# A two-layer gated transformer kernel on one core: a fold padded to full size, another order of memory pools, norms taken by four tiles, and another order of the last stores

## The chip, the cores and the metric

The kernel runs on one core of one Trainium2 chip. All data is fp32. The metric is the device time of one execution in microseconds (us), as the median over several runs. The profile is of one execution and gives the start, the length and the waits of each instruction on each engine: TensorE (PE, with its weight loads as PEld), VectorE (DVE), ScalarE (ACT), GpSimd (POOL) and SyncE (SP), which issues nearly all DMAs.

## The reference

The input x has 8 sequences of 256 rows and 1024 columns. Four sublayers follow one another, each with a layer norm before it and a gate `tanh(g)` behind it:

```python
x = x + tanh(g_xattn[0]) * autocorrelation(layernorm(x), ctx, ctx)     # 8 heads, FFT along the sequence
x = x + tanh(g_ffn[0])   * lora_ffn(layernorm(x), W, b, A, B, gate_w, gate_b)
x = x + tanh(g_xattn[1]) * attention(layernorm(x), ctx, ctx, mask, wq, wk, wv, wo)  # 32 query, 8 kv heads, rope
x = x + tanh(g_ffn[1])   * fourier_ffn(layernorm(x), W_base, b_base, enc0, enc1, coefs0, coefs1, mask0, mask1)
```

The last sublayer is linear in its input. It adds to `x @ W_base.T + b_base` a small-rank update: x goes through encoders of 32 and 8 rows, together 40, then through masked coefficients summed over three sets, and then through an inverse real Fourier transform along the 1024 output columns, all times 0.5. So its whole weight can be made once: `W_base.T + encr.T @ (0.5 * ws.T @ fourier)`, where `encr` is 40 x 1024, `ws` (the masked coefficients, summed) is 1024 x 40, and `fourier` is a constant 1024 x 1024 matrix.

## The kernel before, in words

The work is done in two passes of four sequences each (`NPASS`, `BP`). In a pass, x is held as eight tiles `xt` of 128 rows and 1024 columns (`TT`). The sublayers of a pass follow one another:

- `autocorrelation` does the first sublayer as products with transform matrices (`mats`, `inv`, `inv2`), in turns over sequences and halves of the columns. Beside it, as a generator that is advanced by `fill`, the program makes the keys and values of the attention for the pass (`keys_values`, stored to `kT_d` and `v_d`), and in pass 0, at its end, the weight of the last sublayer (`fold_last_layer`).
- `lora_ffn` does the second sublayer. `prepare` norms a tile (`normed`, L356), transposes it on TensorE (L366), copies it with ScalarE (L367) and multiplies it with the gate and the low-rank factor `ag` (L625).
- `attention` does the third in steps of a block of four tiles and a kv head. Block 0 is tiles 0 to 3, block 1 tiles 4 to 7; the outputs of block 1 (`outputs`, L954) are added to x until the very end of the sublayer.
- `fourier_ffn` does the last with the folded weight, two tiles at a time: `prepare` norms and transposes, `left` makes sums of operands, `project` makes the product of pair m (L1127) while pair m+1 is already prepared, and stores the two tiles. The second tile of a pair holds its rows in reversed order, so it is stored by an indirect DMA of GpSimd with row numbers (L1137); the first goes with a plain DMA of SP (L1136).

The large products use a seven-product scheme for blocks of two by two (`SEVEN`, `left_operands`, `right_operands`, `add_product`). `residual` (L371) adds a scaled product to x on VectorE.

`fold_last_layer` has two products. The first (L302) takes `ws` as its weight, 128 rows by 40 columns, with chunks `ft` of the Fourier matrix, into an accumulator of which 40 rows are used; ScalarE copies these to `dec` (L307). The second (L320) takes `encr` and `dec`, both with 40 rows, and VectorE adds the result to `W_base` (L327), makes the operands of the seven products (L333 to L336), and SP stores them to `w1_d`.

Memory is given out by pools. `big` holds buffers of 4 KB per partition in groups a, b and xn, seven of each, which all sublayers share in turn. Other tiles come from pools that a sublayer opens and closes like a stack: what a later sublayer opens lies at the addresses of what an earlier one closed, and a tile waits for the last reader or writer of the tile that was there. In the first stage of a pass the pools are opened in the order kv1, kv2 (keys and values), ac1, acw, ac2 (autocorrelation), so kv1 lies lowest; the low-rank sublayer's tiles then lie over kv1, kv2, ac1, acw and the start of ac2.

`norm_stats` takes mean and variance of a list of tiles (L349, L350), a root on ScalarE (L351) and a reciprocal (L352). In `fourier_ffn` it is called for tiles 0 to 3 and for tiles 4 to 7 before the first `prepare`.

The order of the instructions on an engine is not the program's. A scheduler decides it when the program is built: it takes what it reckons to be ready, earlier program text first. Each engine then executes its own list in that order, and waits for semaphores.

Of the kernel before, what the change touches and what calls it, by code (L numbers as in the profile page):

```python
# [11 lines left out]
F32 = mybir.dt.float32  # L12
U8 = mybir.dt.uint8
I32 = mybir.dt.int32
AF = mybir.ActivationFunctionType
# [4 lines left out]
P = 128  # L20
B, S, D = 8, 256, 1024
KC = D // P
NPASS = 2
BP = B // NPASS
TT = BP * S // P
HALF = 512
# [5 lines left out]
R1 = 40  # L32
NB = 512
NBT = NB // P
# [12 lines left out]
def flamingo_kernel(ctx: ExitStack, tc: tile.TileContext, a: dict, out: bass.AP):  # L47
    nc = tc.nc
# [4 lines left out]
    big = ctx.enter_context(tc.tile_pool(name="big", bufs=7))  # L53
# [54 lines left out]
    def big_tile(group, shape, name):  # L108
        return big.tile([P, *shape], F32, tag=group, name=name)
# [166 lines left out]
    def fold_last_layer(groups, pools):  # L276


        fp, ps_kv = pools
        group, wt_group = groups  # L280
        co = big_tile(group, [3, KC, R1], "co")
        mk = fp.tile([P, 3, KC, R1], U8, name="mk")
        for e in range(3):
            nc.sync.dma_start(co[:, e], a["coefs"][e].rearrange("(c p) r -> p c r", p=P))
            nc.sync.dma_start(mk[:, e], a["cmask"][e].rearrange("(c p) r -> p c r", p=P))
        encr = big.tile([R1, D], F32, tag=group, name="encr")
        nc.sync.dma_start(encr, a["encr"])
        both = big_tile(group, [2, KC, R1], "both")
        ws, mf = both[:, 0], both[:, 1]
        for e in range(3):  # L290
            nc.vector.tensor_copy(mf, mk[:, e])
            nc.gpsimd.tensor_mul(co[:, e], co[:, e], mf)
        nc.gpsimd.tensor_add(ws, co[:, 0], co[:, 1])
        nc.gpsimd.tensor_add(ws, ws, co[:, 2])
        yield
        dec = big.tile([R1, D], F32, tag=group, name="dec")
        accs = [ps_kv.tile([P, HALF], F32, tag="kv", name="acc") for _ in range(2)]
        for c in range(KC):
            ft = big_tile(group, [2, HALF], "ft")
            nc.sync.dma_start(ft, a["fourier"][c * P : (c + 1) * P, :])  # L300
            for h in range(2):
                nc.tensor.matmul(  # L302
                    accs[h][0:R1, :], ws[:, c, :], ft[:, h, :], start=(c == 0), stop=(c == KC - 1)
                )
            yield
        for h in range(2):
            nc.scalar.activation(  # L307
                dec[:, h * HALF : (h + 1) * HALF], accs[h][0:R1, :], AF.Copy, scale=0.5
            )
        for c in range(KH):  # L310
            wt = []
            for k in range(2):
                rows = slice((k * KH + c) * P, (k * KH + c + 1) * P)
                wt.append(big_tile(wt_group, [2, HALF], "w1in"))
                nc.sync.dma_start(wt[k], a["w1"][rows, :])
            for k in range(2):
                rows = slice((k * KH + c) * P, (k * KH + c + 1) * P)
                for h in range(2):
                    acc = ps_kv.tile([P, HALF], F32, tag="kv", name="acc")
                    nc.tensor.matmul(  # L320
                        acc,
                        encr[:, rows],
                        dec[:, h * HALF : (h + 1) * HALF],
                        start=True,
                        stop=True,
                    )
                    nc.vector.tensor_add(wt[k][:, h, :], wt[k][:, h, :], acc)  # L327
                if k == 0:
                    yield
            q = [[wt[k][:, j, :] for j in range(2)] for k in range(2)]  # L330
            t12, t47 = big_tile(group, [2, HALF], "w_t12"), big_tile(group, [2, HALF], "w_t47")
            nc.sync.dma_start(w1_d[0, :, c, :], q[0][0])
            nc.vector.tensor_sub(t12[:, 0, :], q[0][1], q[0][0])  # L333
            nc.vector.tensor_sub(t47[:, 1, :], q[1][1], q[0][1])
            nc.vector.tensor_sub(t12[:, 1, :], q[1][1], t12[:, 0, :])
            nc.vector.tensor_sub(t47[:, 0, :], t12[:, 1, :], q[1][0])  # L336
            for i, t in ((1, wt[1]), (3, t12), (5, t47)):
                nc.sync.dma_start(w1_d[i : i + 2, :, c, :].rearrange("r p d -> p r d"), t)
            yield
# [15 lines left out]
    def normed(dst, xt, mv, rstd, i):  # L355
        nc.vector.tensor_scalar(  # L356
            dst, xt, mv[:, i, 0:1], rstd[:, i : i + 1], ALU.subtract, ALU.mult
        )
# [731 lines left out]
    def fourier_ffn(p, xt, groups):  # L1090
        with (
            tc.tile_pool(name="f1c", bufs=1, reuse_waits="tile") as w1,
            tc.tile_pool(name="f1", bufs=2, reuse_waits="tile") as w2,
            tc.tile_pool(name="f1_t", bufs=4, space=PSUM) as ps_t,
            tc.tile_pool(name="f1_o", bufs=4, space=PSUM) as ps_o,
        ):
            w = stored_weight(groups, lambda r: w1_d[WEIGHTS.index(r)])

            bias1 = w1.tile([P, D], F32, name="bias1")
            nc.sync.dma_start(bias1, a["b1"].partition_broadcast(P))  # L1100
            nc.vector.tensor_scalar(bias1, bias1, tg_f[1], None, ALU.mult)
            norms = [norm_stats(xt[i * NBT : (i + 1) * NBT]) for i in range(TT // NBT)]

            def prepare(t):
                xn = w2.tile([P, D], F32, tag="xn", name="xn")
                normed(xn, xt[t], *norms[t // NBT], t % NBT)
                xnT = w2.tile([P, KC, P], F32, tag="xnT", name="xnT")
                transposed(xnT, xn, ps_t, "t")
                return xnT

            def left(first, second):
                q = [[s[:, k * KH : (k + 1) * KH, :] for k in range(2)] for s in (first, second)]
                s = [w2.tile([P, KH, P], F32, tag=f"s{i}", name=f"s{i}") for i in (1, 2, 4)]
                return left_operands(nc.vector, q, *s)

            def project(m, ops):
                x = [
                    [xt[m * 2 + i][:, j * HALF : (j + 1) * HALF] for j in range(2)] for i in range(2)
                ]
                part = [w2.tile([P, HALF], F32, tag=f"part{i}", name=f"part{i}") for i in range(2)]  # L1120

                for i in range(2):
                    nc.vector.tensor_add(xt[m * 2 + i], xt[m * 2 + i], bias1)
                for r in SEVEN:
                    po = ps_o.tile([P, HALF], F32, tag="o", name="po")
                    for c in range(KH):
                        nc.tensor.matmul(  # L1127
                            po,
                            ops[r][:, c, :],
                            w[r].chunk(c),  # L1130
                            start=(c == 0),
                            stop=(c == KH - 1),
                        )
                    add_product(r, po, x, tg_f[1], ntg_f[1], part)
                b = p * BP + m
                nc.sync.dma_start(out[b * S : b * S + P, :], xt[m * 2])  # L1136
                nc.gpsimd.indirect_dma_start(  # L1137
                    out,
                    bass.IndirectOffsetOnAxis(ap=rows[:, b : b + 1], axis=0),
                    xt[m * 2 + 1],  # L1140
                    None,
                )

            pending = None
            for m in range(TT // 2):
                got = left(prepare(m * 2), prepare(m * 2 + 1))
                if pending is not None:
                    project(*pending)
                pending = (m, got)
            project(*pending)  # L1150

    for p in range(NPASS):
        ga, gb = ("a", "b") if p % 2 == 0 else ("b", "a")
        xt = [xpool.tile([P, D], F32, tag="x", name="x") for t in range(TT)]
        with (
            tc.tile_pool(name="kv1", bufs=1, reuse_waits="tile") as kw1,
            tc.tile_pool(name="kv2", bufs=2, reuse_waits="tile") as kw2,
            tc.tile_pool(name="ac1", bufs=1, reuse_waits="tile") as c1,
            tc.tile_pool(name="acw", bufs=1, reuse_waits="tile") as aw1,
            tc.tile_pool(name="ac2", bufs=2, reuse_waits="tile") as aw2,  # L1160
            tc.tile_pool(name="ac_dft", bufs=4, space=PSUM) as ps_dft,
            tc.tile_pool(name="ac_cor", bufs=1, space=PSUM) as ps_cor,
            tc.tile_pool(name="ac_out", bufs=1, space=PSUM) as ps_out,
# [28 lines left out]
        with tc.tile_pool(name="at_keep", bufs=1, reuse_waits="tile") as kp:  # L1192
            keep, norms, xops = [], {}, {}
# [163 lines left out]
```

## Time and profile before

| | |
|---|---|
| time, median of 3 runs | 3406.85 us (3405.84 to 3409.39) |
| profiled execution | 3400.72 us, of it 3399.0 us span |
| busy: PE, DVE, ACT, POOL | 3319.6, 2245.2, 859.5, 1355.3 us |
| mean granted clock of PE | 0.989 |
| DMA traffic | 431.72 MB, mean 127 GB/s |
| L302, first product of the fold | 32 instructions, 592 ns each, from 365.1 to 383.2 us |
| L320, second product of the fold | 32 instructions, 890 ns median (589 to 1219), from 385.6 to 412.9 us |
| pass 1 begins its keys on PE | at 1726.4 us |
| last matmul of the attention, pass 0 and pass 1 | 1616.5 and 3280.2 us |

The time of one instruction is from its start to its end; matmuls that follow one another overlap, so 16 instructions of 592 ns take 7.03 us. In a line of the timeline the bracket at the end tells how long the engine stood before it, and what released it. In a table of windows the column behind the five engines is the clock that TensorE was granted, 1.00 being full.

### The profile page before, as it was taken

The page shows a single profiled execution, that of the slowest core. Times are in us where ns is not written, and L with a number is a line of the kernel's source. Part 1 is how long each engine was busy: PE and PEld are TensorE (multiplying, and loading weights), DVE is VectorE, ACT ScalarE, POOL GpSimd, SP SyncE. Part 2 cuts the span into 40 slices and gives each one's busy share as a digit, 9 for nine tenths or more (in the row PEclk, how much of TensorE's full clock was granted, in tenths as well). Part 3 has the DMA queues.
Part 4 walks back from the last instruction along what each step waited for, and adds up shares of the span by engine and source line. Part 5 has one row for each costly group of instructions (what it writes and reads, how often), then busy time and mean ns, then how long its engine had stood idle before and what let it go on. Part 6 is the DMA issues. An engine that isn't in the chain of part 4 may idle for free. (4 is left out here: it accounts for less than half of the span.)

```text
span 3399.0 us, 36938 instructions
## 1 busy us (share of the span) xinstructions
PE 3319.6 (98%) x12784; PEld 2281.0 (67%) x12784; DVE 2245.2 (66%) x4229; ACT 859.5 (25%) x2061; POOL 1355.3 (40%) x1211
## 2 busy tenths in 40 slices
PE   8999999999999999999999999999999999999998
PEld 6676456777667767775467766577767777776754
DVE  7787666877777766665657775566666666666662
ACT  1332111322232322222123321122222323222220
POOL 4655212434443443445345541123443443344432
PEclk9999899999999999999999999999999999999999
DMA  7533625333333333343164333143333333333411
GB/s 273 172 115 117 213 87 176 118 137 133 139 126 129 121 119 120 121 163 103 50 203 153 126 102 131 32 158 123 123 121 121 113 123 115 121 123 122 152 38 50
DMA packets 161864, 431.72 MB, mean 127 GB/s; under 512 B 21476, under 2 KB 56292, under 8 KB 161678
## 3 DMA queue, kind: packets, MB, share of 16 engines
q1 hardware_dynamic: 160526, 425.17, 37.1%
q0 software_dynamic: 1152, 4.19, 0.3%
q8 instruction: 102, 1.67, 0.2%
q14 instruction: 84, 0.69, 0.1%
HBM read 350.66 MB, written 78.64 MB: 126 GB/s over the span
## 5 line engine op out<-in xcount | busy, mean ns | idle before, releaser
L719 POOL TENSOR_TENSOR qT<-rope,rope 128x512 f32<-128x512 f32 x128 | 170.0, 1328 | 866.9 <-DVE rope L718 866.9
L954 PE MATMUL po<-wo,oT 128*128 128x512 f32 x960 | 432.1, 593 | 0.0
L925 PE MATMUL ps_q<-xn,wq 128*128 128x256 f32 x1920 | 428.9, 379 | 0.0
L371 DVE SCALAR_TENSOR_TENSOR x<-po,tg,x 128x512 f32<-128x512 f32 x376 | 269.0, 745 | 201.3 <-PE po L954 70.6
L925 PEld LDWEIGHTS ps_q<-xn,wq 128*128 128x128 f32 x1920 | 364.8, 190 | 50.4 <-PE po L678 0.5
L987 ACT ACTIVATE s<-s,nmx 128x256 f32<-128x256 f32 x512 | 255.9, 500 | 276.5 <-DVE nmx L984 276.0
L982 DVE COPY_PREDICATED s<-keep,ps_s 128x512 f32<-128x512 uint8 x256 | 186.2, 730 | 183.0 <-PE ps_s L973 179.6
L954 PEld LDWEIGHTS po<-wo,oT 128*128 128x128 f32 x960 | 177.4, 190 | 175.6 <-issue 170.5
L954 PE MATMUL po<-wo,oS 128*128 128x512 f32 x640 | 287.7, 592 | 0.3 <-DVE x L371 0.3
L925 PE MATMUL ps_q<-xn_t,wq 128*128 128x256 f32 x1280 | 285.6, 379 | 0.0
L1014 ACT COPY wT<-pt 128x512 f32<-128x512 f32 x256 | 138.2, 590 | 516.3 <-PE pt L1008 516.0
L925 PEld LDWEIGHTS ps_q<-xn_t,wq 128*128 128x128 f32 x1280 | 243.2, 190 | 33.0
L1019 PE MATMUL av<-wT,v 128*128 128x256 f32 x1024 | 247.7, 384 | 3.8 <-ACT wT L1014 3.6
L973 PE MATMUL ps_s<-kT,qT 128*128 128x256 f32 x1024 | 247.9, 379 | 0.0
L1019 PEld LDWEIGHTS av<-wT,v 128*128 128x128 f32 x1024 | 192.5, 191 | 79.2 <-issue 44.0
L996 DVE TENSOR_SCALAR s<-s,tot 128x256 f32<-128x256 f32 x512 | 219.6, 469 | 7.7
L981 POOL MEMSET s<- 128x512 f32 x256 | 129.9, 527 | 222.2 <-PE pt L1008 220.5
L954 PEld LDWEIGHTS po<-wo,oS 128*128 128x128 f32 x640 | 119.0, 190 | 136.6 <-issue 128.9
L973 PEld LDWEIGHTS ps_s<-kT,qT 128*128 128x128 f32 x1024 | 191.6, 190 | 25.3 <-DVE x L371 0.5
L258 POOL TENSOR_TENSOR x<-x,part 128x512 f32<-128x512 f32 x80 | 114.9, 1436 | 213.5 <-ACT part L257 193.6
L984 DVE TENSOR_REDUCE nmx<-s 128x2 f32<-128x512 f32 x256 | 175.0, 685 | 8.3
L716 DVE TENSOR_TENSOR rope<-c,tab_q 128x512 f32<-128x512 f32 x128 | 88.4, 691 | 125.8 <-POOL c L240 119.9
(255 smaller groups left out, 5599.4 us busy)
## 6 DMA issues: line engine op xcount, KB each, us to landing
wq<-in_wq_dram SPq DMA_DIRECT2D x104, 512.0 KB, 3.3
wo<-in_wo_dram SPq DMA_DIRECT2D x104, 512.0 KB, 3.5
wq<-wq_d SPq DMA_DIRECT2D x96, 512.0 KB, 3.2
wo<-wo_d SPq DMA_DIRECT2D x96, 512.0 KB, 3.2
w<-w_d SPq DMA_DIRECT2D x36, 512.0 KB, 4.7
wk<-in_wk_dram SPq DMA_DIRECT2D x26, 512.0 KB, 5.8
wv<-in_wv_dram SPq DMA_DIRECT2D x26, 512.0 KB, 4.4
wk<-wk_d SPq DMA_DIRECT2D x24, 512.0 KB, 4.4
```

What stands on the lines that cost most here:

```text
L371: nc.vector.scalar_tensor_tensor(xs, ps, g, xs, ALU.mult, ALU.add)
L719: nc.gpsimd.tensor_add(dst, t0, t1)
L925: nc.tensor.matmul(ps[:, l, :], wops[r][:, l, c, :], xo[r][:, c, :], start=(c == 0), stop=(c == KH - 1),)
L954: nc.tensor.matmul(po, ops[r][:, h, t * P : (t + 1) * P], wops[r][:, h, :], start=(h == 0), stop=(h == 1),)
L973: nc.tensor.matmul(ps[:, t, :], qT[i, n][:, l, t * P : (t + 1) * P], kT[:, n * S : (n + 1) * S], start=True, stop=True,)
L981: nc.gpsimd.memset(s, MASKED)
L982: nc.vector.copy_predicated(s, keep[b], ps)
L984: nc.vector.tensor_reduce(nmx, s, AX.X, ALU.max, negate=True)
L987: nc.scalar.activation(s[:, t, :], s[:, t, :], AF.Exp, bias=nmx[:, t : t + 1], accum_out=tot[:, t : t + 1],)
L996: nc.vector.tensor_scalar(s[:, t, :], s[:, t, :], tot[:, t : t + 1], None, ALU.mult)
L1014: nc.scalar.copy(wT[i], pt)
L1019: nc.tensor.matmul(av[:, i, :], kv[step][1][:, n * 2 + c, :], wT[i][:, c, :], start=(c == 0), stop=(c == 1),)
```

## The change

It has four parts. In `fold_last_layer` the coefficients go into a zeroed tile `wide` of 128 columns per chunk, `encr` into a zeroed tile of 128 rows, and `dec` has 128 rows, so that both products of the fold are of 128 rows and 128 columns; the mask factors get a buffer of their own. In `fourier_ffn` the statistics are taken in `prepare`, for four tiles when the first of them is due. In `project` the scattered store is issued before the plain one. And the pools of the first stage are opened in another order, the autocorrelation's first, those of keys and values behind them. What is computed is unchanged.

```diff
-        encr = big.tile([R1, D], F32, tag=group, name="encr")
-        nc.sync.dma_start(encr, a["encr"])
-        both = big_tile(group, [2, KC, R1], "both")
-        ws, mf = both[:, 0], both[:, 1]
+
+        encr = big_tile(group, [D], "encr")
+        nc.gpsimd.memset(encr, 0.0)
+        nc.sync.dma_start(encr[0:R1, :], a["encr"])
+        wide = big_tile(group, [KC, P], "wide")
+        nc.gpsimd.memset(wide, 0.0)
+        ws = wide[:, :, 0:R1]
+        mf = big_tile(group, [KC, R1], "mf")
...
-        dec = big.tile([R1, D], F32, tag=group, name="dec")
+        dec = big_tile(group, [D], "dec")
...
-                    accs[h][0:R1, :], ws[:, c, :], ft[:, h, :], start=(c == 0), stop=(c == KC - 1)
+                    accs[h], wide[:, c, :], ft[:, h, :], start=(c == 0), stop=(c == KC - 1)
...
-                dec[:, h * HALF : (h + 1) * HALF], accs[h][0:R1, :], AF.Copy, scale=0.5
+                dec[:, h * HALF : (h + 1) * HALF], accs[h], AF.Copy, scale=0.5
...
-            norms = [norm_stats(xt[i * NBT : (i + 1) * NBT]) for i in range(TT // NBT)]
+            norms = {}
 
             def prepare(t):
+                if t % NBT == 0:
+                    norms[t // NBT] = norm_stats(xt[t : t + NBT])
...
-                nc.sync.dma_start(out[b * S : b * S + P, :], xt[m * 2])
                 nc.gpsimd.indirect_dma_start(
                     out,
                     bass.IndirectOffsetOnAxis(ap=rows[:, b : b + 1], axis=0),
                     xt[m * 2 + 1],
                     None,
                 )
+                nc.sync.dma_start(out[b * S : b * S + P, :], xt[m * 2])
...
-            tc.tile_pool(name="kv1", bufs=1, reuse_waits="tile") as kw1,
-            tc.tile_pool(name="kv2", bufs=2, reuse_waits="tile") as kw2,
             tc.tile_pool(name="ac1", bufs=1, reuse_waits="tile") as c1,
             tc.tile_pool(name="acw", bufs=1, reuse_waits="tile") as aw1,
             tc.tile_pool(name="ac2", bufs=2, reuse_waits="tile") as aw2,
+            tc.tile_pool(name="kv1", bufs=1, reuse_waits="tile") as kw1,
+            tc.tile_pool(name="kv2", bufs=2, reuse_waits="tile") as kw2,
```

## The prediction

> **What bounds the kernel now.** I read the page first, then the windows of five microseconds around each place where the clock or TensorE's busy share dips, then the timelines of TensorE, VectorE and GpSimd there.
>
> ```profile
> PE 3319.6 (98%) x12784; PEld 2281.0 (67%) x12784; DVE 2245.2 (66%) x4229; ACT 859.5 (25%) x2061; POOL 1355.3 (40%) x1211
> PEclk9999899999999999999999999999999999999999
> ```
>
> TensorE is busy for 3319.6 of 3399.0 us. A change that takes no matmul away can win only two things: the 79 us in which TensorE stands, and the time in which it runs at a lowered clock. The chain of waits says the same, nearly all of it is TensorE. So I looked for dips. The fifth slice is the only one with a granted clock below nine tenths:
>
> ```profile
> 375.00:380.00 5.00, 5.00 (x12) 1.41 (x11) 2.30 (x4) 0.00 (x0) 2.02 (x3) 1.00 0.29 105
> ...
> 400.00:405.00 5.00, 5.00 (x9) 2.38 (x9) 3.18 (x5) 0.00 (x0) 0.00 (x0) 0.50 0.60 230
> ...
> 410.00:415.00 5.00, 3.96 (x5) 1.11 (x4) 3.62 (x8) 0.00 (x0) 0.00 (x0) 0.50 0.70 263
> ...
> 420.00:425.00 5.00, 5.00 (x25) 5.00 (x25) 2.98 (x9) 1.73 (x4) 0.00 (x0) 0.50 1.02 328
> ```
>
> Columns: window, length, busy time of PE, PEld, DVE, ACT and POOL, then granted clock, DMA share, GB/s. From 400 us TensorE is busy all the time and yet gets half its clock. TensorE's timeline names what runs there (an fp32 matmul shows as two instructions):
>
> ```profile
> 378.45 5.34 PE L302 MATMUL acc<-ft,both 128*40 128x512 f32 x12
> ...
> 401.51 12.45 PE L320 MATMUL acc<-dec,encr 40*128 40x512 f32 x14
> 417.69 1.94 PE L366 MATMUL pt<-ident,xn 128*128 128x128 f32 x8 [3.73 <-DVE sc L636]
> ```
>
> The fold's first product, 128 rows by 40 columns, holds the full clock (0.44 us each). Its second, 40 rows by 128 columns, is in train when the clock falls (by windows of one microsecond between 398 and 399) and runs at 0.89 us each. Every other dip that I looked into follows a stand of 2.5 us or more; this one alone falls with TensorE busy.
>
> Next, three places where TensorE stands. The change of stage in pass 1, from the key and value projection to the low-rank layer:
>
> ```profile
> 2080.22 1.09 PE L366 MATMUL pt<-ident,xn 128*128 128x128 f32 x8 [1.56 <-DVE xa L640]
> 2085.92 3.68 PE L625 MATMUL pa<-ag,xnT 128*128 128x68 f32 x16 [4.61 <-ACT xnT L367]
> ```
>
> ```profile
> 2083.94 0.81 DVE L356 TENSOR_SCALAR xn<-x,mv,rstd 128x1024 f32<-128x1024 f32 x1 [3.77 <-DMA v_d<-v]
> ```
>
> The norm of tile 1 writes where the last v tile lay, so VectorE waits for its store; ScalarE's root and copies stand behind that, and TensorE behind them. The last layer of both passes starts with a stand too (pass 1 shown):
>
> ```profile
> 3280.85 0.73 DVE L371 SCALAR_TENSOR_TENSOR x<-po,tg,x 128x512 f32<-128x512 f32 x1
> 3281.50 1.28 DVE L349 BATCH_NORM_STATS2 st<-x 128x6 f32<-128x512 f32 x2
> ...
> 3282.81 0.76 DVE L356 TENSOR_SCALAR xn<-x,mv,rstd 128x1024 f32<-128x1024 f32 x1
> ...
> 3386.59 1.41 DVE L371 SCALAR_TENSOR_TENSOR x<-po,tg,x 128x512 f32<-128x512 f32 x2 [2.62 <-PE po L1127]
> 3390.03 0.75 DVE L371 SCALAR_TENSOR_TENSOR x<-po,tg,x 128x512 f32<-128x512 f32 x1 [2.02 <-PE po L1127]
> ```
>
> ```profile
> 3283.71 1.94 PE L366 MATMUL pt<-ident,xn 128*128 128x128 f32 x8 [3.55 <-DVE xn L356]
> 3285.52 2.07 PE L1127 MATMUL po<-w,xnT 128*128 128x512 f32 x2
> ```
>
> The norm of tile 0, whose own statistics were taken long before, sits behind statistics of tiles 4 to 7. And the end: the last residual is done at 3390.8, the plain store goes then, and the scattered store starts only when that has landed, 4.8 us before the span ends.
>
> ```profile
> 3394.21 0.97 POOL L1137 DMA_INDIRECT out_dram<-x,rows  x1 [11.17 <-DMA out_dram<-x]
> ```
>
> **The change part by part.** The sum is made against the profiled execution, 3400.72 us (span 3399.0 and 1.7 around it), which lies 6.1 us below the median of the runs, 3406.85.
>
> *Padding of the fold.* Rows of the second product go from 40 to 128, the columns of the first likewise. No matmul is added; 128 or 40 columns cost the same 592 ns row (L302 and L954), and the longer weight load (117 to 190 ns) lies beside a matmul of 512 columns. Two memsets of 128x1024 come to GpSimd, about 1.05 us each by the 527 ns of a 128x512 one; GpSimd idles 5.99 us before its add at 340.27, after the buffer of encr came free at 335.3. If that cover is gone they cost 2.1 us of GpSimd. One more big buffer is held (mask factors apart), so a fourier chunk may load a step later; the factors were ready at 350 and are used at 365. I cost these at nothing.
>
> What it may win is the clock. Half clock lasts from 398.6 to 425.4, 26.8 us with a stand of 3.7, so 11.5 us of TensorE's time are lost: upper end 12. Lower end: nothing, if the array's monitor does not count rows of zeros. Here a rule speaks against the change. The Trainium skill ("TensorE: Matmul & The Clock Gate", the parts on the clock gate and on why it matters) says that the gate goes by how busy the PE has been, and that a matmul with K=32 takes the time of one with K=128. By it 40 rows at 100% busy would hold the clock and padding would win 0. The rows above say that 40 rows at 5.00 of 5.00 got 0.50 while 128 rows by 40 columns got 1.00; the measurement decides, so I expect the full clock. Then VectorE is next: from 396.85 it has 22 fold operations of about 0.61 us and 0.6 us of small ones left, 14 us, and ends at 410.9 in place of 416.75. That is 5.9 us. The transposes and gate matmuls behind it (417.7 to 425.4, at half clock) win another 3.9 by the clock alone, but the copies and table load of ScalarE between them (1.28 us) then show; I count 1.6. Gain 7.5, bounds 0 and 12.
>
> *Pool order.* The low-rank layer's tiles now lie over the autocorrelation's pools, not over those of keys and values. Pass 1: their last reader is the matmul of L532 that ends at 2076.9, not the v store at 2083.9. Norm 0 can follow the residual (2078.4), norm 1 at once, transposes of both by 2081, root and copies by about 2082.4. What is late next is the load of ag, issued at 2079.89 behind the v store; by its row (5.4 us to landing) it is there at 2085.3, or at about 2082.5 if it is issued at 2077. So the gate matmuls come 1 to 3.5 us earlier, tile 1's transposes (1 us) fall into the wait, and of the 2.7 us lost to half clock behind the stand about half goes. I take 4.5, bounds 0 and 8. Pass 0: ag and bl now lie over the transform matrices, so they can't load at 371.6 but at about 389.5, after the last L532. SP issues nothing between 372.4 and 387.8, so nothing is queued behind; ag lands at 395 and the first use was at 394.88, in a stretch with DMA at 0.78 to 0.95. Loss 1, bounds 0 and 5. The start of pass 1 and attention: the same bottom addresses are covered as before; nothing.
>
> *Norms by four.* The stand and half clock at the start of the last layer cost 3.94 + 0.98 + 0.97 = 5.9 in pass 0 and 3.55 + 0.98 + 1.19 + 1.04 = 6.8 in pass 1 (transposes 1.94 against 0.96 for eight, products 1.85 and 2.07 against 0.88, transposes 2.95 against 1.91). With no statistics ahead of it norm 0 runs at 3279.3 or, behind the last residual, at 3281.6: TensorE stands 0.1 to 2.2 us, and about 0.6 us for the first copies. (A stand of 2.47 us before 613.9 was followed by half clock, one of 2.19 before 2051.7 was not, so I count none.) I leave 1.75 per pass: gain 12.7 - 3.5 = 9.2, bounds 4 and 12. The statistics of tiles 4 to 7 (eight of 0.65, four of 0.2, 6 us, and a root with its 1.28 us table load) must now fit before the transposes of tile 4 at 3314.2; VectorE idles about 8 us between 3298 and 3314, which hides them.
>
> *Scattered store first.* Its tile is ready at 3388.0 (second residual of the pair at 3386.59), the plain one at 3390.8. Both write the same tensor, so the second still waits: scatter lands at 3388.1 + 3.9 = 3392.0, plain store 3.4 later, 0.9 to the end: 3396.3 against 3399.0. Gain 2.7, bounds 0 and 3.9. SP now stands at the plain store instead of GpSimd at the scatter, about 2 us longer; behind it are pass 1's x, wk and ctx loads, whose first uses are 15 us or more away.
>
> Sum: 7.5 + 4.5 - 1 + 9.2 + 2.7 = 22.9, so 3377.8 for a like execution, 3384 for the median.
>
> **The rivals.** (a) *The clock stays halved*: zeros are not counted. For it: no row here shows a matmul padded with zeros. Against it: the fall with 40 rows, none with 40 columns. Sum 15.4: 3391.5. (b) *The orders hardly move*: what each engine issues first is fixed by a scheduler, and norm 0 may stay where it is because its tile opens late; then 3 us of the tail and little else remain, 3402. For it: VectorE had idle time from 3253 on and norm 0 did not use it. (c) *Slower*: norm 0 stays and the statistics of tiles 4 to 7 land directly in front of norm 4. Place: VectorE before the transposes at 1649.8 and 3314.2. Price: 6 of statistics, 1.6 on ScalarE, 1.2 for reciprocal and norm, some 3 of half clock, 11.8 per pass and 23.6 in all, against 13.7 from the other parts: 3417. It decides once more than 7 us per pass are exposed. Against it: 8 us of idle VectorE there.
>
> **How the numbers follow.** Main forecast 0.62, (a) 0.2, (b) 0.12, (c) 0.06. About 0.2% (6.8 us) is what a measurement of this kernel can tell from no change. The main case and (a) are faster, and a third of (b): 0.86; the rest of (b) is the same, 0.08; (c) 0.06. The range: all upper ends together (12, 8, 12, 3.9) would give 3371, which is unlikely at once; 3373 to 3398 holds the main case, (a), and the better edge of (b).
>
> **What would show it.** Right: L320 at 592 ns with 128 rows and a clock of 1.00 from 395 to 425; the norm of tile 1 in pass 1 without the wait for the v store; the first transposes of the last layer less than 2.5 us behind the last L954; the scatter near 3388 before the plain store. Wrong: L320 at 890 ns; gate matmuls in pass 0 waiting for ag; a stand before the transposes of tile 4.

## The result, and the profile after

The changed kernel takes 3390.79 us (median of 6 runs, 3386.70 to 3399.65), the kernel before in the same session 3407.11 (3405.84 to 3409.39). The ratio is 0.9959, 95% interval 0.9948 to 0.9969: 14.0 us less (11 to 18), where the prediction had 23. (The two medians are 16.3 us apart; I go by the ratio.) The time lies in the predicted range, but the sum behind it does not hold in all its terms. The runs after spread over 13 us, those before over 3.6. The profiled execution after took 3396.83 us, its span is 3395.0, so it is one of the long ones, while the one before (3400.72) is shorter than any of the six runs before. The two profiles are therefore only 3.9 us apart: they show where time went, and not the 14 us.

The page of the changed kernel, first the busy times, then the granted clock in 40 slices:

```profile
PE 3314.1 (98%) x12784; PEld 2279.1 (67%) x12784; DVE 2252.4 (66%) x4229; ACT 859.7 (25%) x2061; POOL 1354.6 (40%) x1213
PEclk9999999999999999999999999999999999999999
```

The dip in the fifth slice is gone, but TensorE's busy time fell by only 5.5 us. To see where the rest is, I cut the TensorE timelines of all profiled executions at the same matmuls. Kernels e1 to e12 are those of the experiments; times in us.

| stretch | before | after | e1 padding | e2 pools | e6 pools pass 0 | e8 | e10 |
|---|---|---|---|---|---|---|---|
| first matmul to first fold matmul | 359.2 | 368.2 | 360.4 | 369.5 | 367.4 | 362.0 | 361.0 |
| fold to last attention matmul, pass 0 | 1251.5 | 1249.0 | 1244.4 | 1262.3 | 1262.5 | 1245.5 | 1244.9 |
| last layer, pass 0 | 109.0 | 108.2 | 109.0 | 110.1 | 110.0 | 111.3 | 105.8 |
| to the last L532 matmul, pass 1 | 351.4 | 351.6 | 358.7 | 354.3 | 358.5 | 356.6 | 351.1 |
| to the first gate matmul, pass 1 | 9.0 | 5.4 | 8.8 | 4.8 | 9.0 | 5.2 | 5.2 |
| to the last attention matmul, pass 1 | 1194.2 | 1194.3 | 1194.2 | 1194.5 | 1195.4 | 1193.0 | 1194.6 |
| last layer, pass 1 | 109.8 | 107.3 | 109.8 | 108.6 | 108.8 | 105.6 | 107.3 |
| from the last matmul to the end | 9.0 | 5.3 | 9.0 | 9.0 | 9.0 | 5.3 | 5.3 |

The columns before and after differ in both directions: 9 us are lost ahead of the fold, five stretches win 1 to 4, and two (up to the last L532 matmul of pass 1, and its attention) do not move. A stretch of one execution is not exact either. From the fold to the attention, e3, e4 and e7, whose edits do not touch that stretch, take 1254.9 to 1255.9 us where the profile of before has 1251.5: the clock of the fold's second product falls 27 to 32 us after the first fold matmul there, and 33.5 in before. Up to the last L532 matmul of pass 1 the kernels lie between 349.7 and 358.7. I go through the stretches in the order of the prediction. In kernels that have the change, lines are 4 to 6 higher than before (in e11 by 2): L302 and L320 (fold) are L306 and L324, L366 is L370, L356 is L360, L371 is L375, L669 is L673, L1127 is L1133, L584 is L588.

*Fold.* Windows (columns as in the prediction: length, busy time of the five engines, then clock, DMA share, GB/s), and TensorE's timeline behind them:

```profile
400.00:405.00 5.00, 4.38 (x20) 2.58 (x20) 5.00 (x9) 1.08 (x2) 0.00 (x0) 1.00 0.89 277
410.00:415.00 5.00, 3.38 (x8) 1.05 (x7) 4.98 (x9) 0.00 (x0) 0.00 (x0) 1.00 1.02 376
```

```profile
414.92 2.33 PE L324 MATMUL acc<-dec,encr 128*128 128x512 f32 x4 [1.12 <-DVE w1in L331]
...
424.21 4.50 PE L673 MATMUL po<-w,xnT 128*128 128x512 f32 x6 [2.00 <-DVE w1in L331]
...
432.84 6.70 PE L673 MATMUL po<-w,xnT 128*128 128x512 f32 x8 [3.13 <-DMA w<-in_w_dram]
```

The clock is 1.00 through the second product, and VectorE is busy for 4.98 to 5.00 of 5 us: it is the next limit, as predicted. The last fourteen instructions of this product take 1057 to 1058 ns (median, from start to end) in all six profiles with 40 rows and 592 to 593 in all eight with 128. But then TensorE waits 2.00 us for a fold operation of VectorE and 3.13 us for the load of the next weight. Neither wait was there before.

*Pool order in pass 1.* TensorE's timeline:

```profile
2085.01 1.09 PE L370 MATMUL pt<-ident,xn 128*128 128x128 f32 x8 [0.50 <-DVE xn L360]
2088.18 3.65 PE L629 MATMUL pa<-ag,xnT 128*128 128x68 f32 x16 [2.08 <-DMA ag<-in_ag_dram]
```

The wait for the v store is gone, and the load of ag is what comes last, as predicted.

*Last layer, pass 1.* VectorE, then TensorE:

```profile
3282.55 0.69 DVE L353 BATCH_NORM_STATS2 st<-x 128x6 f32<-128x512 f32 x1
3283.17 0.73 DVE L375 SCALAR_TENSOR_TENSOR x<-po,tg,x 128x512 f32<-128x512 f32 x1
3283.82 1.53 DVE L360 TENSOR_SCALAR xn<-x,mv,rstd 128x1024 f32<-128x1024 f32 x2
```

```profile
3284.77 2.85 PE L370 MATMUL pt<-ident,xn 128*128 128x128 f32 x16 [2.29 <-DVE xn L360]
```

The norm now follows the last residual, with no statistics between them. The stand is 2.29 us in place of 3.55, and half clock still follows it (16 transposes in 2.85 us; at full clock they take 1.91).

*The end.* GpSimd's scatter, then SP's plain store:

```profile
3388.06 0.98 POOL L1142 DMA_INDIRECT out_dram<-x,rows  x1 [5.23 <-DVE x L375]
```

```profile
3391.45 0.33 SPq L1148 DMA_DIRECT2D out_dram<-x  x1
```

*Ahead of the fold.* One VectorE instruction that takes 0.43 us in the median, the end of GpSimd's work beside it, and the matmul that waits for what is queued behind it:

```profile
121.64 11.23 DVE L588 SCALAR_TENSOR_TENSOR w<-took,ex 128x256 f32<-128x256 f32 x1
```

```profile
130.05 2.54 POOL L158 TENSOR_TENSOR wv_s<-wv,wv_s 128x512 f32<-128x512 f32 x2
```

```profile
134.71 2.07 PE L536 MATMUL po<-re,inv 128*128 128x512 f32 x2 [6.79 <-DVE x L375]
```

That is most of the 9 us. No step of the prediction has anything at this place.

### The profile page after: what moved, and what is told of

Its sections match the earlier page's. It is cut to its first block, busy times and chain, and to the rows that moved or that the text cites. A ratio compares the mean times of both kernels' runs of the same rounds, so it can differ in the third digit from the quotient of the medians.

```text
span 3395.0 us, 36926 instructions
## 1 busy us (share of the span) xinstructions
PE 3314.1 (98%) x12784; PEld 2279.1 (67%) x12784; DVE 2252.4 (66%) x4229; ACT 859.7 (25%) x2061; POOL 1354.6 (40%) x1213
## 5 line engine op out<-in xcount | busy, mean ns | idle before, releaser
L375 DVE SCALAR_TENSOR_TENSOR x<-po,tg,x 128x512 f32<-128x512 f32 x376 | 269.1, 745 | 196.0 <-PE po L958 70.5
L258 POOL TENSOR_TENSOR x<-x,part 128x512 f32<-128x512 f32 x80 | 109.1, 1364 | 229.5 <-ACT part L257 222.1
L263 POOL TENSOR_TENSOR x<-x,part 128x512 f32<-128x512 f32 x80 | 104.7, 1310 | 172.7 <-DVE part L375 157.0
```

Source lines behind the costliest of these rows:

```text
L375: nc.vector.scalar_tensor_tensor(xs, ps, g, xs, ALU.mult, ALU.add)
```

## The experiments

All ratios are to the kernel before, run on the same chip in turn; 0.001 is 3.4 us.

**Each part alone (e1 to e4), on the kernel before.**

```diff
# e1: the hunks of the fold
...
+        wide = big_tile(group, [KC, P], "wide")
...
+        dec = big_tile(group, [D], "dec")
...
# e2: the hunk of the pools
-            tc.tile_pool(name="kv1", bufs=1, reuse_waits="tile") as kw1,
-            tc.tile_pool(name="kv2", bufs=2, reuse_waits="tile") as kw2,
             tc.tile_pool(name="ac1", bufs=1, reuse_waits="tile") as c1,
...
+            tc.tile_pool(name="kv1", bufs=1, reuse_waits="tile") as kw1,
+            tc.tile_pool(name="kv2", bufs=2, reuse_waits="tile") as kw2,
# e3: the hunk of prepare()
+                if t % NBT == 0:
+                    norms[t // NBT] = norm_stats(xt[t : t + NBT])
# e4: the hunk of project()
-                nc.sync.dma_start(out[b * S : b * S + P, :], xt[m * 2])
                 nc.gpsimd.indirect_dma_start(
...
+                nc.sync.dma_start(out[b * S : b * S + P, :], xt[m * 2])
```

> Only the padding of the fold, on the kernel before. Theory (read from the two traces): the clock is 1.00 from 398 to 425 us and L324 runs at 592 ns, but the last load of w1in is issued some 20 us later because one big buffer more is held, so the last fold additions and the first load of the next weight come late: 2 to 4 us are left, about 3404. Rival 1 (the step of the prediction): 7.5 us are won, about 3399.5, with no wait for a load behind the fold. Rival 2: the 9 us that the changed kernel lost ahead of the fold (one VectorE instruction of 11.23 us) come with the padding; then the first fold matmul is some 9 us later than before and the kernel is 5 us slower, 3412.

> Only the pool order, on the kernel before. Theory: in pass 1 the gate matmuls of the low-rank layer come about 2.4 us earlier against the last L532 matmul (the wait for the v store is gone, the load of ag is late next), and in pass 0 they come up to 1 us later: 1.5 to 2.5 us faster, about 3405. Rival 1 (the prediction): 4.5 - 1 = 3.5 faster, 3403.5. Rival 2: the buffers of the first stage lie elsewhere and VectorE's long instruction under GpSimd's train of additions at 121 to 133 us comes with this part: then the first fold matmul is 9 us later and the kernel is 6 us slower, 3413.

> Only the norms of the last layer by four tiles, on the kernel before. Theory (from the two traces): some of the statistics of tiles 4 to 7 stay ahead of the last residual, TensorE stands 2.3 to 2.8 us before the first transposes of the last layer in place of 3.5 to 3.9, and about 1 us in pass 0 and 2.5 us in pass 1 are won: 3.3 faster, 3403.5. Rival 1 (the prediction): 9.2 us, 3397.6, with stands under 2.2 us and the full clock behind them. Rival 2: nothing, as the scheduler puts the statistics where they were; 3407.

> Only the scattered store ahead of the plain one, on the kernel before. Theory (from the two traces): the tail behind the last matmul goes from 9.0 to 5.2 us, 3.8 us faster, 3403. Rival 1 (the prediction): 2.7 us, 3404.2. Rival 2: nothing at all, if the two stores share the queue's completion; 3407.

| run | median, us | ratio | 95% interval | us against before |
|---|---|---|---|---|
| e1 padding | 3397.45 | 0.9975 | 0.9965 to 0.9985 | -8.5 |
| e2 pools | 3408.98 | 1.0007 | 0.9998 to 1.0016 | +2.4 |
| e3 norms | 3403.03 | 0.9991 | 0.9982 to 0.9999 | -3.1 |
| e4 store | 3405.18 | 0.9994 | 0.9986 to 1.0002 | -2.0 |

The four add up to -11.2, inside the interval of the whole. The padding is worth about what the prediction gave it, not the 2 to 4 us that I read from the trace of after: my theory for e1 was wrong. For e2 it was wrong as well: its second rival, the long instruction, came, though +2.4 us is not clear of zero. e3 came out as its theory had it; e4 cannot tell 3.8 from 2.7. The late load that I had put down to the padding's extra buffer does not come with it. SP's queue in e1, then in after:

```profile
372.45 0.42 SPq L1211 DMA_DIRECT2D ag<-in_ag_dram  x1
...
393.25 0.34 SPq L319 DMA_DIRECT2D w1in<-in_w_dram  x1
```

```profile
397.66 0.38 SPq L1213 DMA_DIRECT2D ag<-in_ag_dram  x1
...
415.91 0.50 SPq L319 DMA_DIRECT2D w1in<-in_w_dram  x1
...
427.20 3.91 SPq L119 DMA_DIRECT2D w<-in_w_dram  x6
```

In e1 the last w1in load goes 27 us after the first fold matmul, in after 42 us. e2 has it late too (50 us), with no padding in it. So it belongs to the pool order, and so does the instruction of 11 us in the profiles: e2 has one of 11.53 us at 123.67, while e1, e3 and e4 have none there.

What the padding leaves: the fold's last wait is for VectorE, and a stand of 3.7 us behind it still drops the clock. TensorE and windows of e1:

```profile
411.59 1.94 PE L370 MATMUL pt<-ident,xn 128*128 128x128 f32 x8 [3.74 <-DVE sc L640]
```

```profile
405.00:410.00 5.00, 2.25 (x4) 0.59 (x4) 4.98 (x12) 0.00 (x0) 0.00 (x0) 0.98 1.02 379
410.00:415.00 5.00, 3.41 (x16) 3.22 (x16) 4.70 (x18) 2.26 (x4) 0.00 (x0) 0.50 1.01 345
```

**The pool order by pass (e6, e7), and the change without it (e5) or with it in pass 1 alone (e8).**

```diff
+        sizes = {"kv1": 1, "kv2": 2, "ac1": 1, "acw": 1, "ac2": 2}
+        order = list(sizes) if p == 1 else ["ac1", "acw", "ac2", "kv1", "kv2"]   # e6
+        order = list(sizes) if p == 0 else ["ac1", "acw", "ac2", "kv1", "kv2"]   # e7, e8
...
+                n: st.enter_context(tc.tile_pool(name=n, bufs=sizes[n], reuse_waits="tile"))
+                for n in order
```

> The changed kernel without the pool order (padding, norms by four and scattered store only). Theory (from the single runs: padding -8.5 to -9, norms -3.3, store -3.2 to -3.8, pool order +2.4): the pool order costs and does not win, so this is faster than the changed kernel: 3407 - 15 = 3392 or less, with the last w1in load where it was, no late load of the next weight and no VectorE instruction of 11 us at 122 us. Rival (the step of the prediction): the pool order wins 3.5, so this is slower than the changed kernel, 3394.5 by its measured 3390.8.

> Only the pool order, in pass 0 alone, on the kernel before. Theory: all of its cost lies here. The tile of ag opens late, the last w1in load is queued behind stores and goes some 20 us later, and the first load of the next weight behind that: from the first gate matmuls to the attention 6 to 8 us are lost; an 11 us VectorE instruction at 122 us may add 9. 3413 without, 3422 with. Rival (the prediction): 1 us lost, 3408.

> Only the pool order, in pass 1 alone, on the kernel before. Theory: what it wins lies here, 3.6 to 4.2 us between the last L532 matmul of pass 1 and the first gate matmul, and nothing before that differs: 3403. Rival 1 (the prediction): 4.5, 3402.5. Rival 2: the gain is given back in pass 1 as the cost is in pass 0: 3407.

> The changed kernel with the pool order in pass 1 alone. Theory: all gains without the cost in pass 0: 9 for the padding, 3.3 norms, 3.5 store, 4 pool order = 19.8 less than 3407: 3387, 4 us ahead of the changed kernel. Rival: the parts share their stands, so no more than the changed kernel, 3391.

| run | median, us | ratio | 95% interval | us against before |
|---|---|---|---|---|
| e5 change without pool order | 3395.50 | 0.9956 | 0.9943 to 0.9970 | -15 |
| e6 pool order, pass 0 alone | 3422.02 | 1.0030 | 1.0020 to 1.0040 | +10.2 |
| e7 pool order, pass 1 alone | 3404.24 | 0.9977 | 0.9967 to 0.9988 | -7.8 |
| e8 change, pool order in pass 1 alone | 3391.91 | 0.9942 | 0.9928 to 0.9955 | -19.8 |

(On this chip the kernel before ran at 3411.56; only the ratios compare with the first table.) One edit, two passes, opposite signs. The theory held for e6 and e8. For e7 the stretch to the first gate matmul is 5.0 us in place of 9.0, as expected; its ratio says more than these 4 us, but 4 is at the edge of its interval. e5 tells nothing against after (0.9956 and 0.9959), since the two halves of the pool order nearly cancel. In e6 the fold to the end of the attention takes 1262.5 us, in e7 1254.9: the late loads cost 7.6 us without padding (11.0 against the 1251.5 of before). With it they cost 3.6 (1249.0 in after, 1245.5 in e8). TensorE's stands for them in e6, which e7 does not have:

```profile
442.96 3.70 PE L669 MATMUL po<-w,xnT 128*128 128x512 f32 x8 [2.47 <-DMA w<-in_w_dram]
...
453.88 6.50 PE L669 MATMUL po<-w_t,s 128*128 128x512 f32 x8 [3.61 <-DVE w_t L140]
```

**Rows alone (e11).** The first product stays at 40 columns, the second gets 128 rows.

```diff
...
+        nc.gpsimd.memset(encr, 0.0)
...
+        nc.gpsimd.memset(dec, 0.0)
...
+                dec[0:R1, h * HALF : (h + 1) * HALF], accs[h][0:R1, :], AF.Copy, scale=0.5
```

> Only the rows of the second fold product padded (decoder and encoder factors 128 rows, 88 of them zero), on the kernel before; the first product stays at 40 columns. Theory: the fall of the clock comes from 40 rows in use, so all of the gain of the padding lies here: the second product at 592 ns, the clock 1.00 from 398 to 425 us, 9 us faster, ratio 0.9975. Rival: the clock needs both, or counts the columns of the first product; then it stays at 0.50 from 400 us on and nothing is won, 1.000.

The ratio is 0.9963 (0.9949 to 0.9976), 12.6 us less: all of the padding's gain, as the theory said. Windows and TensorE's timeline:

```profile
400.00:405.00 5.00, 4.23 (x9) 1.16 (x7) 4.98 (x9) 0.00 (x0) 0.00 (x0) 1.00 0.95 360
```

```profile
401.54 3.18 PE L322 MATMUL acc<-dec,encr 128*128 128x512 f32 x6 [0.42 <-DVE w1in L329]
```

With 88 rows of zeros the clock holds, although TensorE is busy for less of the window (4.23 us) than before (5.00 at half clock). A part for the columns of the first product does not show.

**GpSimd's trains (e9, e10, e12).** A train is a row of instructions with no gap between them. In after, GpSimd has one from 114.1 to 132.6 us; the instruction of 11.23 us ends when this train ends, and the others of its line between 150 and 360 us take 0.4 to 1.1 us. Half of the train are the sums of the wv factors. e9 is the changed kernel with these on VectorE. e10 is e8 with the sums of the context operands on VectorE, for all blocks after the first. e12 has both.

```diff
-                eng = Short(nc.gpsimd if kind == "wv" else nc.vector)      # e9, e12
+                eng = Short(nc.vector)
-            cops.update(right_operands(Short(nc.gpsimd), q, *t))           # e10, e12
+            cops.update(right_operands(Short(nc.vector), q, *t))
```

> The changed kernel, with the sums of the wv factors (eight additions of 1.25 us each on GpSimd for each half, in the train from 117 to 133 us) made by VectorE instead. Theory: VectorE's instruction of 11.2 us at 122 us is shut out while GpSimd runs without a gap; with the train broken none is longer than 2 us, the first fold matmul comes back from 374 to 366 or 368, and the kernel is 6 to 8 us faster than the changed one: 3384 beside 3407. Rival 1: the length comes from where the pool order puts the instruction's tiles; then 11 us stay and the kernel is the same, 3391. Rival 2: eight more additions of 0.7 us each on VectorE cost what the train did.

> The kernel with all parts and the pool order in pass 1 alone, with the sums of the context operands for all blocks after the first made by VectorE instead of GpSimd (the train from 1608 to 1618 us that held one norm for 3.6 us, and those at 1880 to 1920 us). Theory: the two norms at the start of the last layer in pass 0 take 1.5 us in place of 4.4, the stand of TensorE goes from 5.2 to 2.3 us, the 9.08 us instructions of L467 go too, and the kernel is 3 to 6 us faster than without this: ratio to before 0.9930. Rival: VectorE gets 24 additions of 0.7 us more, four of them right before these norms, and the kernel is the same or slower, 0.9942 or more.

> The kernel of the run before last (all parts, pool order in pass 1 alone, context sums on VectorE), with the sums of the wv factors made by VectorE too. It asks why moving them won nothing in the median of the changed kernel although the 11 us instruction was gone. Theory A: the move itself costs VectorE what the train cost; here, where the profile shows no instruction of 11 us at 122 us to be won, it is 5 to 8 us slower than without it, ratio to before 0.9937. Theory B: the move costs nothing, and the 11 us instruction is not in most executions of the changed kernel; here it is the same, 0.9918, or up to 2 us faster.

| run | median, us | ratio | 95% interval |
|---|---|---|---|
| e9 after, wv sums moved | 3398.15 | 0.9962 | 0.9948 to 0.9975 |
| e10 e8, context sums moved | 3382.78 | 0.9918 | 0.9905 to 0.9932 |
| e12 e8, both moved | 3383.01 | 0.9914 | 0.9901 to 0.9928 |

e10 is the clear case. At the start of the last layer of pass 0, e8 has a worse stand than the kernel before. VectorE, GpSimd and TensorE of e8:

```profile
1614.50 4.40 DVE L360 TENSOR_SCALAR xn<-x,mv,rstd 128x1024 f32<-128x1024 f32 x2
```

```profile
1615.13 2.50 POOL L158 TENSOR_TENSOR cx_t<-cx_t,cx 128x512 f32<-128x512 f32 x2
```

```profile
1618.33 3.65 PE L370 MATMUL pt<-ident,xn 128*128 128x128 f32 x16 [5.17 <-DVE xn L360]
```

Two norms of 0.76 us take 4.40 us; the first of them takes 3.68, to 1618.18, and ends 0.6 us after GpSimd's train of context sums does (1617.63). With the sums on VectorE, the same two lines of e10:

```profile
1613.20 1.52 DVE L360 TENSOR_SCALAR xn<-x,mv,rstd 128x1024 f32<-128x1024 f32 x2
```

```profile
1614.15 1.94 PE L370 MATMUL pt<-ident,xn 128*128 128x128 f32 x16 [2.43 <-DVE xn L360]
```

The last layer of pass 0 goes from 111.3 to 105.8 us, and the stretch after it from 356.6 to 351.1 (where other context sums were moved as well). That is 11 us in these two executions, and 8 by the ratios (whose intervals still overlap, 0.9928 to 0.9955 and 0.9905 to 0.9932). For the first stretch e12 agrees (107.5; after, e3, e5, e8 and e9, which have norms by four and the sums on GpSimd, take 108.2 to 111.3). For the second the move is not shown to be the cause: before, after and e9 have 351.4 to 351.9 there with the sums on GpSimd. There e8 gets half clock after much the same stands that before passed at full clock (see the last section). e10 and e12 are the fastest kernels of the study, 28 us below the kernel before and about 14 below the change as it was made.

e9 missed. Its profile shows the instruction at 0.42 us:

```profile
125.67 0.42 DVE L588 SCALAR_TENSOR_TENSOR w<-took,ex 128x256 f32<-128x256 f32 x1
```

The first fold matmul comes at 367.1 in place of 374.0, so without the train the instruction is short, with the tiles where the changed kernel has them. But the train alone is not enough. The kernel before has the same train, from 113.2 to 132.0 us, and its VectorE instructions of that line take 0.67 and 1.37 us under it; the longer one, and GpSimd beside it:

```profile
129.54 1.37 DVE L584 SCALAR_TENSOR_TENSOR w<-took,ex 128x256 f32<-128x256 f32 x1
```

```profile
128.12 1.29 POOL L240 TENSOR_TENSOR v<-w,m 128x512 f32<-128x512 f32 x1
129.37 2.67 POOL L158 TENSOR_TENSOR wv_s<-wv,wv_s 128x512 f32<-128x512 f32 x2
```

What the pool order of pass 0 adds, another moment of the start or another place of the tiles, was not separated. And that execution of e9 (3390.94 us) is the shortest of five; the other four took 3398.0 to 3398.6, and the median won nothing. e12 says that the move itself costs nothing (0.9914 and 0.9918). So either the 11 us are not in most executions of the changed kernel, or e9's other executions lost the same elsewhere. For the first speaks that all three profiled executions with the long instruction lie at the upper end of their runs: after second of six, e2 (3420.62) first of 13, e6 (3428.30) first of nine. Only a profile shows the instruction, and there is one of each kernel, so this stays open, and with it how much of e6's 10 us is the train.

## Why the prediction was right, and where it was not

| step | predicted, us | profiled stretches | run alone, by ratio |
|---|---|---|---|
| padding of the fold | 7.5 | 7.1 (before to e1), 10.5 (e7 to e1) | 8.5 (5.1 to 11.9), e11 12.6 |
| pool order, pass 1 | 4.5 | 4.0 (before to e7) | 7.8 (4.1 to 11.2) |
| pool order, pass 0 | -1 | -7.6 late loads (e7 to e6), -3.6 with the padding (e8 to after), and up to -9 by the long instruction | -10.2 (-6.8 to -13.6) |
| norms by four | 9.2 | 0.8 + 2.5 (before to after) | 3.1 (0.3 to 6.1) |
| scattered store first | 2.7 | 3.7 (before to after) | 2.0 (-0.7 to 4.8) |
| sum | 22.9 | | all together 14.0 (11 to 18) |

**Padding: right in mechanism and in its main term.** Full clock with 128 rows, VectorE next: from the start of the second product to the transposes behind it e1 takes 26.0 us and before 32.1, so 6.1, where 5.9 were forecast. The last term, 1.6 for those transposes and gate matmuls at full clock, did not come: the stand of 3.7 us stays, and e1 runs them at 0.50 as before. That the stretch wins 7.1 all the same is luck in part, since e1 also begins the second product 1.2 us sooner after the first, which no step had. The rule weighed there (the Trainium skill, "TensorE: Matmul & The Clock Gate", that the gate follows how busy TensorE was and that a short K takes the time of a full one) would have won nothing; e11, with 592 ns and a clock of 1.00, decides for the rows. The buffer that I costed at nothing did cost nothing: in e1 the last w1in load is no later against the fold than before (27 and 28 us). The rival of a clock that stays halved falls, and by the clock alone. By the time alone it would have stood: its sum was 3391.5, nearer to the measured 3390.79 than the 3384 of the main forecast. The short norms and pass 0 happened to take away about what the padding brought.

**Pool order, pass 1: right**, down to ag as the next late thing (2.08 us of wait).

**Pool order, pass 0: the step that failed.** It had ag landing later and said that SP issues nothing in that time, "so nothing is queued behind". The step counted what stands behind ag at its old place alone, and the sign that it named, gate matmuls of pass 0 waiting for ag, did not show: in after they wait 0.24 us, for ScalarE. What counts is where ag goes: SP issues in one fixed order, ag went from 372 to 398 us, and the last w1in load and the first loads of the next weight went with it to later places in that order. Why the scheduler placed w1in so was not tried. The step had its upper bound at 5; without padding the late loads alone cost 7.6, with it 3.6.

**Norms by four: mechanism right, size off by a factor of three.** Two terms were mis-sized. First, "I leave 1.75 per pass": the norm stays behind the last residual, so the stand is 0.73 of residual, 0.76 of norm and the hand-overs, 2.29 us, the upper end of what I had given. Second, "I count none" for half clock, from two stands of 2.47 and 2.19 us. There is no such limit: a stand of 2.29 us at this same place is followed by half clock in after, e3, e5, e9, e10 and e12 (2.52 to 3.50 us for 16 transposes) and by full clock in e8 (1.94), and one of 2.43 us in pass 0 of e10 by full clock. In pass 0 it was neither: the norms were held by GpSimd's context sums, 2.93 us for two in after, and the gain there was 0.8. The rival of orders that hardly move has a part in this, since norm 0 did not pass the last residual. Its reason, a tile that opens late, is not shown: in after the norm begins as soon as VectorE is done with the residual, with no wait in between. Why the scheduler left the norm behind the residual was not tried.

**Slower by statistics before tile 4: did not happen.** They ran in VectorE's idle time, and the transposes of tile 4 start at 3314.00 us with no stand before them.

**Store: right** in place and order (scatter at 3388.06, predicted 3388.0); it landed half a microsecond sooner than by the row that I took.

The total is 9 us short of its sum: the norms gave 6 us less, and pass 0's pool order took 3 more with the padding beside it (9 more alone, by ratio). Padding (e1), store (e4) and, by the trace, pass 1's pool order came within about 1 us of their terms. The range held because it reached down to a gain of 9 us.

## What to carry over

A change of pools is a change of every wait that their tiles had, in each pass, so price it per pass: here the same edit won 4 us in one pass and, without the padding, lost 8 or more in the other. When a DMA's tile opens later, ask what comes behind it in its queue's new order, not only what was behind it in the old one. And before a stand is charged to the engine that released it, compare the duration of its last instruction with the median of its kind: here one that was almost five times too long (3.68 us for 0.76) pointed to another engine, GpSimd.

## What the runs showed of the hardware

*A matmul with 40 of 128 rows at 100% busy got 0.50 of the clock, one with 88 rows of zeros added got 1.00* (before against e11); the fall comes in all six profiles with 40 rows and in none of the eight with 128. So here the clock followed the rows in use, rows of zeros among them, and not the busy time.

*A VectorE instruction can be shut out for a whole train of GpSimd instructions.* L588, with both inputs in SBUF, took 11.23 us in after, 11.53 in e2 and 11.28 in e6, under an unbroken train, and 0.42 in e9, where the train was broken; the addition to `ke` (L467 before) took 9.08 us in e1, e2, e4, e6, e7 and e11. The Trainium skill ("SBUF — State Buffer", Who interferes with whom) says that a VectorE instruction with two SBUF inputs contends with GpSimd's reads, and that whoever issues first has the shared pair for that whole instruction. The kinds agree. The length does not: the wait went through some nine GpSimd instructions in a row, while in the profile of before an instruction of the same line took 1.37 us under the same train.

*The same stand of 2.29 us cost the clock in six profiles and not in a seventh.* A longer one can leave it: before the L532 matmuls of pass 1 TensorE stands 3.69 us in the profile of before and goes on at full clock (1.02 us for the second pair), and 3.29 us in e8, at half clock (1.92). The Trainium skill ("TensorE: Matmul & The Clock Gate", Part 1) has the gate watch a window that runs freely, so that its answer depends on where in the window the work falls. That this holds for a stand too is my inference: the runs fit it, but none shows the window.
